# A fused convolution-attention and mixture-of-experts kernel: four taps a step, another plan for the last batch's expert tiles, and a combination that runs on into the tail

## The chip, the cores and the metric

The kernel runs on one core of a Trainium2 chip. Time is device time in microseconds of one execution; several executions are given by their median. The core has a matrix engine (TensorE; PE in the profile, its weight loads PEld), a vector engine (VectorE, DVE), an activation engine (ScalarE, ACT), GpSimd (POOL) and a queue processor (SyncE, SP) that issues most DMAs. Each engine works through its own instructions in the order in which the program lists them.

## The reference

The input x is 8 images of 256 channels, 32 x 32 pixels. Layer 0 is a deformable attention with a learned position bias; layer 1 is a token attention with sigmoid weights and a mixture of 8 experts, two per token:

```python
# layer 0, on the group-normalised image, residual added
q = gconv1x1(x, wq)
off = tanh(pointwise(gelu(depthwise_6x6_stride_4(q)))) * 4        # 36 taps
vgs = normalize(grid + off)                                       # 8 x 8 sample points
kv = grid_sample(x, vgs);  k, v = gconv1x1(kv, wk), gconv1x1(kv, wv)
pos = grid_q - vgs
bias = mlp3(sign(pos) * log1p(abs(pos)))                          # 2 -> 64 -> 64 -> 1, for 1024 x 64 pairs
out = softmax(q k / 8 + bias) v;  x = x + w_out out
# layer 1, on tokens (1024 a batch, 256 wide), each part on layer-normalised tokens
t = t + sigmoid(t Wq t^T) t
for the two best experts e of a token:  t = t + weight_e * (gelu(t w1[e]) w2[e])
```

## The kernel before

**The main loop.** The costliest part is the bias network: its second layer (`second_layer`, L486) and third layer (`third_layer`, L506) on TensorE, its first layer (`first_layer`, L468) on GpSimd and VectorE in turn, the rectifications on ScalarE and VectorE. The loop `for n in range(NB * TURNS)` (L1122) walks through it in 64 turns a batch, `b, i = divmod(n, TURNS)`, with two second layers a turn and a third layer every other turn. All other work is written as Python generators, and each turn takes a few steps from them. So the order of work on every engine is written out by hand, by these turns; `in_order` (L76) fixes it as the order in which each engine runs. Only the scatters of routed rows may change places, and only among themselves between two other instructions of their engine.

**What a turn steps, in this order.**
- `mix(b, i, 0)` (L1145): expert steps, ahead of the bias layers.
- The bias layers, and with them the preparation of the next block of bias inputs, eight turns a block (L1139 to L1161): `scale()` when `n % 8 == 3`, `second()` and `hold(0)` when it is 4, `hold(1)` when it is 6. `hold` copies half of the block into a PSUM tile (`held_nb`) that the first layer on VectorE reads; the tile `still` that holds it is also where the taps (`shared`) accumulate and where small statistics live.
- `side.step` (L1163): the softmax of this batch (`softmax`, L533) and the preparation of the next batch's image (`prep`, L241): group statistics, normalising, query projection, the 36 taps of the depthwise convolution as VectorE additions in PSUM (L286 to L295, three taps a step), GELU, offsets, the pair table `fd` sent to DRAM, sampling weights, transposes (L382), the sampling matmuls (L394), keys and values (L409 to L421).
- `advance(mains)` (L1171): one step of each running token attention. `attention(b, ...)` (L606) returns two generators. `upper` starts at turn 53 of its own batch, `rest` at turn 0 of the next batch. `rest` ends with routing (`route`, L812) and then 16 scatters (L793, indirect DMAs on GpSimd's queue) that put the rows into the slots of their experts; after the last it appends the batch's `experts` to the list `mixtures`.
- `mix(b, i, 1)` (L1172): expert steps, behind the others.
- `step(sums)` (L1173): one step of the oldest `combine` (L991).

**Experts and combination.** `experts(b, rt)` (L911) works in rounds of 256 slots: 12 rounds for batches 0 to 6 (two tiles of 128 slots each, possibly of two experts), 15 for batch 7 (tiles of 256). A round takes three steps: second layer of the round before last (L945), its bias (L950) and the DMA of the rows to `ys` (L951); then fetches of rows (`xl`, L925) and weights (L932) and the first layer of the round before (L966, L974); then the transposes of this round's rows (L985, L987). A batch of 12 rounds takes 41 steps; after the last, its `combine` is appended to `sums`. `combine` has 22 steps: steps 0 to 15 each gather the rows of one of two experts for 128 tokens (`gs`, L1019, an indirect DMA on GpSimd's queue, which needs all rows in `ys`), steps 3 to 18 add them with their weights on VectorE (L1011), and steps 8, 12, 16 and 20 transpose a quarter of the result on TensorE (L1002), copy it on ScalarE and send it out (L1005).

**When expert steps fall due** is in `mix` (L1095). In batches 2 to 6, the experts of the batch two before (b - 2) get a step at turn 26, two steps in each of the 13 odd turns of `ODD` (31 to 55) and one in the turn after each; the 41st comes at turn 9 of the batch after. In the last batch (b = 7) three steps (`whole()`, L1116) are taken at once after turn 9, in turns that are odd or divisible by three, until batch 5's experts are through; batch 6's start at turns 62 and 63.

**The tail** (L1176 to L1189) follows the last turn: a loop steps batch 7's `rest` until it has ended, and takes a `whole()` of batch 6's experts in odd iterations while no attention tiles run, and in each iteration from the second of the routing on. Then a loop over batch 7's experts takes `whole()` and one `step(sums)` an iteration, and a last loop takes what is left of `sums`.

Of the kernel before, what the change touches and what calls it, by code (L numbers as in the profile page):

```python
# [67 lines left out]
TURNS = STEPS // 2  # L68
# [35 lines left out]
def tile_conv_attn_hybrid(ctx: ExitStack, tc: tile.TileContext, x, par, qw, w1, w2_, cst, out):  # L104
    nc = tc.nc
    NB = x.shape[0]
# [16 lines left out]
    def big(name):  # L123
        return t8.tile([P, 2, N], F32, tag="t8", name=name)
# [21 lines left out]
    def xin(b):  # L146
        return x[b].rearrange("(k p) h w -> p k (h w)", p=P)
# [11 lines left out]
    def par_(name):  # L159
        return pr_[:, PAR[name]]  # L160
# [80 lines left out]
    def prep(b, xb, st):  # L241
# [44 lines left out]
        for t in range(KS * KS):  # L286
            ky, kx = divmod(t, KS)
            row = (26, 0, 9, 18, 27, 1)[ky]
            tap = qp[:, row : row + 8].rearrange("p r k x -> p (r k) x")[:, :, kx : kx + 29 : 4]
            if t == 0:  # L290
                nc.vector.tensor_scalar(oc, tap, dw[:, 0:1], par_("dwb"), ALU.mult, ALU.add)
            else:
                nc.vector.scalar_tensor_tensor(oc, tap, dw[:, t : t + 1], oc, ALU.mult, ALU.add)
            if t % 3 == 2:
                yield  # L295
        oa = one.tile([P, 2, 8, 8], F32, name="oa")
        nc.scalar.activation(oa.rearrange("p k y x -> p y k x"), oc.rearrange("p (y k) x -> p y k x", k=2), AF.Gelu)
# [134 lines left out]
    def terms(b, k, h, part):  # L432
        number = 4 * k + 2 * h + part
        fd = sts[b]["fd"].rearrange("k (s r) f -> k r s f", r=2)
        ta = abpool.tile([P, 16, 2, 32], F32, name="ta")
        nb = abpool.tile([P, 16, 2, 16], F32, name="nb")
        nc_ = abpool.tile([P, 2, 8, 16], F32, name="nc")
        taf = ta.rearrange("p s g x -> p s (g x)")
        nbf = nb.rearrange("p s g y -> p s (g y)")
        ss = slice(part * 16, (part + 1) * 16)  # L440
        for r in range(2):
            rs = slice(64 * r, 64 * r + 64)
            nc.sync.dma_start(out=taf[rs], in_=fd[k, r, ss, 0:64].partition_broadcast(64))
            nc.sync.dma_start(out=nbf[rs], in_=fd[k, r, ss, 64 + 32 * h : 96 + 32 * h].partition_broadcast(64))

        def scale():
            nc.scalar.activation(taf, taf, AF.Identity, bias=par_("cb1"), scale=par_("w1x"))
            nc.scalar.activation(nbf, nbf, AF.Identity, scale=nw1y)

        def second():  # L450
            cps = [psum("cp") for _ in range(2)]
            for r, g in ((0, 0), (1, 1), (0, 1), (1, 0)):
                rs, gs = slice(64 * r, 64 * r + 64), slice(64 * g, 64 * g + 64)
                nc.tensor.matmul(
                    cps[r][gs, 0:128], lhsT=par_("w2")[rs, gs], rhs=nb[rs, 1::2, g, :],
                    start=True, stop=True, tile_position=(64 * r, 64 * g),
                )
            for r in range(2):
                nc.scalar.activation(  # L459
                    nc_[:, r].rearrange("p s y -> p (s y)"), cps[r][:, 0:128], AF.Identity, bias=ncb2,  # L460
                )

        def hold(half):
            nc.scalar.copy(held_nb[:, 4 * half : 4 * half + 4], nb[:, 8 * half + 1 : 8 * half + 8 : 2])  # L464

        return (ta, nb, nc_, b, number), scale, second, hold

    def first_layer(terms_, n):  # L468
        ta, nb, nc_, of, number = terms_
        h1 = hpool.tile([P, 2, 16, W], F32, name="h1", bufs=6)  # L470
        a = ta[:, n].unsqueeze(2).to_broadcast([P, 2, 16, W])
        b = nb[:, n].unsqueeze(3).to_broadcast([P, 2, 16, W])
        if second_form(of, number, n):
            b = held_nb[:, n // 2].unsqueeze(3).to_broadcast([P, 2, 16, W])
            nc.vector.tensor_tensor(h1, a, b, ALU.max)  # L475
            return h1, nc_[:, :, n // 2]
        nc.gpsimd.tensor_tensor(h1, a, b, ALU.subtract)  # L477
        return h1, None

    def rectify(h1, nc_):  # L480
        if nc_ is None:
            nc.scalar.activation(h1, h1, AF.Relu)  # L482
# [542 lines left out]
    class Side:  # L1025
# [5 lines left out]
        def step(self, both=True):  # L1031
            busy = False
            if self.waiting and not (sorting and self.busy):
                busy = self.busy
                self.busy = next(self.waiting[0], None)
                if self.busy is None:
                    self.waiting.pop(0)
                    self.busy = True
            if self.left and both and not busy:
                self.left = next(self.prep, self) is not self  # L1040
# [21 lines left out]
    h2s, side = [], None  # L1062

    mains, mixtures, sums = [], [], []

    def place(t):
        b, s = divmod(t, STEPS)
        return b, s // 64, s // 32 % 2

    def logits(t):  # L1070
        b, k, h = place(t)
        ss = third_layer(sts[b], k, h, t // 4 % 8, h2s[:4])
        del h2s[:4]
        if ss is None:
            return None
        if (k, h) == (0, 0):
            os_[b] = big("o")
        if (k, h) == (1, 1):
            sts[b]["last"] = ss
        else:  # L1080
            return softmax(sts[b], k, h, ss, os_[b], psum)

    def residual(b):
        xres[b] = big("x")
        nc.sync.dma_start(out=xres[b], in_=xin(b))
# [8 lines left out]

    def mix(b, i, part):  # L1095
        of = mixtures[0][0] if mixtures else NB
        if b == NB - 1 and of >= b - 2:
            if part and (i >= TURNS - 2 if of == b - 1 else i > 9 and (i % 2 or i % 3 == 0)):
                whole()
        elif of == b - 2:  # L1100
            if not part:
                due = i in ODD
            else:
                due = i == 26 or i in ODD or i - 1 in ODD
            if due:
                step(mixtures)
        elif of == b - 3 and i == 9 and not part:
            step(mixtures)

    ODD = (31, 33, 35, 37, 39, 41, 43, 45, 47, 49, 51, 53, 55)  # L1110

    def step(what):
        if what and next(what[0][1], what) is what:
# [2 lines left out]
    def whole():  # L1116
        of = mixtures[0][0] if mixtures else NB
        for _ in range(3):
            if mixtures and mixtures[0][0] == of:
                step(mixtures)  # L1120

    for n in range(NB * TURNS):  # L1122
        b, i = divmod(n, TURNS)
        turn = i
        if i == 0:
            steps = iter(())
            if b + 1 < NB:
                xb = big("xb")
                nc.sync.dma_start(out=xb, in_=xin(b + 1))
                steps = prep(b + 1, xb, sts[b + 1])  # L1130
            side = Side(steps)
        if b == 0 and i in (8, 16):
            nc.sync.dma_start(
                out=xss[i // 8 - 1].rearrange("(t p) c -> p t c", p=P),
                in_=zero.unsqueeze(1).to_broadcast([P, ROWS // P, C]),
            )
        if i == 46:
            residual(b)
        coming_ = (n // 8 + 1) * 16  # L1139
        if coming_ < total and n % 8 == 0:  # L1140
            b_, k_, h_ = place(coming_)
            coming, scale, second, hold = terms(b_, k_, h_, coming_ // 16 % 2)
        if n % 8 == 6 and coming_ < total:
            table = coming
        mix(b, i, 0)  # L1145
        new = []
        if n + 2 < NB * TURNS:
            new = [first_layer(table, (2 * n + 4 + r) % 16) for r in range(2)]
        h1s += new
        h2s += [second_layer(*h1s.pop(0)) for _ in range(2)]  # L1150
        for h in new:
            rectify(*h)
        ready = n % 2 == 0 and n and logits(2 * n - 1)
        if coming_ < total:
            if n % 8 == 3:
                scale()
            elif n % 8 == 4:
                second()
                hold(0)
            elif n % 8 == 6:  # L1160
                hold(1)  # L1161
        if i > 4 and not (sorting and i % 2):
            side.step(i > (8 if b else 4))  # L1163
        if ready:
            side.waiting.append(ready)
        if i == 0 and b:
            mains.append((b, below))
        elif i == 53:
            above, below = attention(b, sts[b], os_.pop(b), {})
            mains.append((b, above))  # L1170
        advance(mains)  # L1171
        mix(b, i, 1)  # L1172
        step(sums)  # L1173
        if i == TURNS - 1:
            side.finish()
    logits(total - 1)  # L1176
    mains.append((b, below))
    n = sorted_ = 0
    while mains:
        advance(mains)  # L1180
        if sorted_ or not attending and n % 2:
            whole()
        sorted_ = sorted_ or sorting
        n += 1
    while mixtures:
        whole()
# [111 lines left out]
```

## Time and profile before

| what | us |
|---|---|
| median of 3 runs | 3100.75 |
| lowest, highest | 3093.69, 3102.71 |
| the profiled execution | 3095.55 |
| its span, first to last instruction | 3093.7 |
| TensorE busy in it | 2816.0 (91%) |
| VectorE, ScalarE | 1897.3, 1899.3 (61% each) |
| GpSimd | 1382.0 (45%) |
| mean granted TensorE clock | 0.979 of full |

A turn begins in the trace where TensorE begins a turn's 16 matmul records of line L490. By that, the batches begin at these times:

| batch | begins at, us | length, us |
|---|---|---|
| 0 | 72.8 | 256.4 |
| 1 | 329.2 | 323.6 |
| 2 | 652.8 | 358.3 |
| 3, 4, 5, 6 | 1011.1, 1370.6, 1730.2, 2089.8 | 359.6 each |
| 7 | 2449.3 | 372.7 |
| tail | 2822.0 | 271.7 |

How to read the profile: engines are busy or idle; idle time is put down to whatever ended it, written `<-engine tile line`. A waiting instruction holds up all later instructions of its engine. Idle time of an engine counts only where the work that ends last had to wait for it. The names in a row, `out<-in`, are those of the program's tiles.

### The profile page before, as it was taken

Reading aid. Unit: us, or ns where it says so; the run is one execution under the profiler, and the core shown is the slowest. Engines: PE = TensorE matmul, PEld = TensorE weight load, DVE = VectorE, ACT = ScalarE, POOL = GpSimd, SP = SyncE. Lnnn points to the kernel's source line nnn. Section 1 sums busy time; section 2 is a strip of 40 time slices with the busy share of each in tenths; the row PEclk is TensorE's granted clock in tenths of the full one; section 3 lists DMA queues with packets and bytes.
Section 4 is the critical chain, followed back from the end, with each engine's and each line's share of the span. In section 5 each row is a group of like instructions: output and inputs, shape, how many; then the busy total and the mean of one; then the engine's idle time right before and its main releaser. Section 6 shows DMA issues by size and latency. Waiting matters only on the chain. (4 is left out here: it accounts for less than half of the span.)

```text
span 3093.7 us, 51788 instructions
## 1 busy us (share of the span) xinstructions
PE 2816.0 (91%) x19592; PEld 1393.8 (45%) x19592; DVE 1897.3 (61%) x2968; ACT 1899.3 (61%) x2735; POOL 1382.0 (45%) x945
## 2 busy tenths in 40 slices
PE   3989998899999999999999999999999998989965
PEld 2223453334454454444445444554545455425754
DVE  4887667766765676656765567656775553593112
ACT  3776656666576656756576666766577665665322
POOL 2555434644344543545535464445435443472123
PEclk7999999999999999999999999999999999999988
DMA  3321111210373124712265124731256154433377
GB/s 102 89 46 35 21 28 28 60 38 15 103 209 100 42 65 133 208 47 57 81 175 155 48 57 111 215 91 44 64 142 201 32 147 141 129 93 96 120 232 225
DMA packets 428298, 311.23 MB, mean 101 GB/s; under 512 B 284432, under 2 KB 368656, under 8 KB 428048
## 3 DMA queue, kind: packets, MB, share of 16 engines
q1 hardware_dynamic: 415472, 273.14, 31.5%
q0 software_dynamic: 12288, 33.57, 3.4%
q8 instruction: 155, 2.54, 0.3%
q10 hardware_dynamic: 288, 1.20, 0.1%
q14 instruction: 95, 0.78, 0.1%
HBM read 239.93 MB, written 67.90 MB: 100 GB/s over the span
## 5 line engine op out<-in xcount | busy, mean ns | idle before, releaser
L477 POOL TENSOR_TENSOR h<-ta,nb 128x1024 f32<-128x1024 f32 x512 | 980.8, 1918 | 1123.3 <-PE h2p L490 1001.9
L490 PE MATMUL h2p<-h,pr__101 64*64 64x512 f32 x8192 | 1011.9, 605 | 82.0 <-DVE h L498 55.5
L496 ACT ACTIVATE h<-h2p,pr__101 128x1024 f32<-128x1024 f32 x512 | 570.9, 1115 | 485.8 <-PE h2p L490 485.4
L498 DVE TENSOR_TENSOR h<-h2p,nc 128x1024 f32<-128x1024 f32 x512 | 625.3, 1221 | 316.4 <-PE h2p L490 303.9
L475 DVE TENSOR_TENSOR h<-ta,still 128x1024 f32<-128x1024 f32 x512 | 620.1, 1211 | 46.8 <-ACT still L464 42.8
L482 ACT ACTIVATE h<-h 128x1024 f32<-128x1024 f32 x512 | 537.8, 1051 | 13.5 <-POOL h L477 13.2
L490 PEld LDWEIGHTS h2p<-h,pr__101 64*64 64x64 f32 x8192 | 254.4, 132 | 607.3 <-issue 284.1
L517 PE MATMUL sim<-h,pr__101 128*32 128x512 f32 x4096 | 496.6, 603 | 0.0
L950 DVE TENSOR_TENSOR yt<-yp,w 128x512 f32<-128x512 f32 x99 | 68.5, 692 | 379.6 <-PE yp L945 333.3
L517 PEld LDWEIGHTS sim<-h,pr__101 128*32 128x32 f32 x4096 | 107.5, 109 | 362.8 <-issue 362.7
L723 PE MATMUL ap<-qt,tn 128*128 128x256 f32 x1024 | 252.4, 390 | 4.1 <-ACT sg L741 2.6
L733 PE MATMUL vp<-tt,sg 128*128 128x256 f32 x1024 | 233.0, 381 | 3.6 <-ACT nc L459 3.3
L723 PEld LDWEIGHTS ap<-qt,tn 128*128 128x128 f32 x1024 | 185.7, 191 | 88.4 <-issue 40.4
L945 PE MATMUL yp<-w,ht 128*128 128x256 f32 x792 | 201.2, 398 | 25.5 <-ACT ht L974 7.0
L1019 POOL DMA_INDIRECT gs<-ys,slot x128 | 129.7, 1014 | 193.1 <-DVE xc L1011 51.5
L966 PE MATMUL hp<-xg,w 128*128 128x128 f32 (+1 forms) x1464 | 200.0, 289 | 12.1 <-ACT xg L987 4.4
L733 PEld LDWEIGHTS vp<-tt,sg 128*128 128x128 f32 x1024 | 193.5, 190 | 36.9 <-issue 5.7
L966 PEld LDWEIGHTS hp<-xg,w 128*128 128x128 f32 x1464 | 183.4, 193 | 45.7 <-issue 23.5
L745 DVE TENSOR_TENSOR x<-x,vp 128x512 f32<-128x512 f32 x64 | 44.0, 688 | 256.3 <-PE vp L733 256.3
L974 ACT ACTIVATE ht<-hp,w 128x128 f32<-128x128 f32 (+1 forms) x366 | 108.6, 377 | 146.7 <-PE hp L966 127.2
L945 PEld LDWEIGHTS yp<-w,ht 128*128 128x128 f32 x792 | 147.2, 196 | 61.4 <-ACT ht L974 13.9
L741 ACT ACTIVATE sg<-ap 128x512 f32<-128x512 f32 x128 | 76.5, 598 | 143.8 <-PE ap L723 131.9
(273 smaller groups left out, 2556.9 us busy)
## 6 DMA issues: line engine op xcount, KB each, us to landing
w<-in_w SPq DMA_DIRECT2D x183, 384.0 KB
w<-in_w SPq DMA_DIRECT2D x183, 257.0 KB
ta<-fd SPq DMA_DIRECT2D x128, 256.0 KB
xl<-xs SPq DMA_DIRECT2D x99, 256.0 KB
ys<-yt SPq DMA_DIRECT2D x99, 256.0 KB
nb<-fd SPq DMA_DIRECT2D x128, 128.0 KB
xb<-in_x SPq DMA_DIRECT2D x8, 1024.0 KB
x<-in_x SPq DMA_DIRECT2D x8, 1024.0 KB
```

What stands on the lines that cost most here:

```text
L475: nc.vector.tensor_tensor(h1, a, b, ALU.max)
L477: nc.gpsimd.tensor_tensor(h1, a, b, ALU.subtract)
L482: nc.scalar.activation(h1, h1, AF.Relu)
L490: nc.tensor.matmul(h2p[gs, r, :], lhsT=par_("w2")[rs, gs], rhs=h1[rs, g].rearrange("p y x -> p (y x)"), start=True, stop=True, tile_positi ...
L496: nc.scalar.activation(h2, h2p, AF.Relu, bias=par_("cb2"))
L498: nc.vector.tensor_tensor(h2.rearrange("p r (y x) -> p r y x", x=W), h2p.rearrange("p r (y x) -> p r y x", x=W), nc_.unsqueeze(3).to_broad ...
L517: nc.tensor.matmul(sim[32 * q : 32 * q + 32, :], lhsT=par_("z3")[:, 15 - m : 47 - m], rhs=h2s[2 * u + q // 2][:, q % 2, :], start=False, s ...
L723: nc.tensor.matmul(ap[:, u, :], lhsT=tn[:, k, m0 : m0 + P], rhs=qt[:, k, quarter(q)], start=(k == 0), stop=(k == 1),)
L733: nc.tensor.matmul(vp[:, i, :], lhsT=sgs[s][:, u, i * P : (i + 1) * P], rhs=tt[:, 2 * todo[n - 2 + s][1] + u, :], start=(s == u == i == 0) ...
L945: nc.tensor.matmul(yp[:, s, :], lhsT=ht[:, f, s * P : (s + 1) * P], rhs=f2[:, s * several // 2, f * C : (f + 1) * C], start=(f == 0), stop ...
L966: nc.tensor.matmul(hp[:, f, us], lhsT=f1[:, u, k * C + f * P : k * C + (f + 1) * P], rhs=xg[:, k, us], start=(k == 0), stop=(k == 1),)
L1019: nc.gpsimd.indirect_dma_start(out=got[m][:, c, :], out_offset=None, in_=yv[:, :], in_offset=bass.IndirectOffsetOnAxis(ap=slot[:, c, m : m ...
```

## The change

Four edits are made, and no instruction is added or taken away; only their order changes.

1. The taps of `prep` yield after every fourth tap, so that the 36 taps take 9 steps and no longer 12. `prep` gets no step in turns after 44 whose number is 3 or 4 modulo 8.
2. `hold(0)` is issued one turn later, in the turn with `n % 8 == 5`.
3. In the last batch `mix` follows the same pattern as in the others, with a list of its own, `LATE`: batch 4's last step comes at turn 1; batch 5's experts start with one step in turn 2, take steps at turns 3, 4, 7 and 8, and then the odd turns 35 to 55 and the ones after them, with the last step in turn 57. Batch 6's experts take no step in the main loop any more; they start in the tail.
4. The tail's first loop takes a `step(sums)` in each iteration. Batch 5's combination, which begins in turn 57, goes on there, and batch 6's begins there when its experts have ended.

```diff
@@ prep @@
-            if t % 3 == 2:
+            if t % 4 == 3:
                 yield
@@ mix @@
         of = mixtures[0][0] if mixtures else NB
-        if b == NB - 1 and of >= b - 2:
-            if part and (i >= TURNS - 2 if of == b - 1 else i > 9 and (i % 2 or i % 3 == 0)):
-                whole()
-        elif of == b - 2:
-            if not part:
-                due = i in ODD
-            else:
-                due = i == 26 or i in ODD or i - 1 in ODD
-            if due:
+        odd, first_, last = (LATE, 2, 1) if b == NB - 1 else (ODD, 26, 9)
+        if of == b - 2:
+            if i in odd or part and (i == first_ or i - 1 in odd) or b == NB - 1 and i == odd[-1] + 2 and not part:
                 step(mixtures)
-        elif of == b - 3 and i == 9 and not part:
+        elif of == b - 3 and i == last and not part:
             step(mixtures)
     ODD = (31, 33, 35, 37, 39, 41, 43, 45, 47, 49, 51, 53, 55)
+    LATE = (3, 7, 35, 37, 39, 41, 43, 45, 47, 49, 51, 53, 55)
@@ the main loop @@
             elif n % 8 == 4:
                 second()
+            elif n % 8 == 5:
                 hold(0)
             elif n % 8 == 6:
                 hold(1)
         if i > 4 and not (sorting and i % 2):
-            side.step(i > (8 if b else 4))
+            side.step(i > (8 if b else 4) and not (i > 44 and i % 8 in (3, 4)))
@@ the tail @@
         if sorted_ or not attending and n % 2:
             whole()
         sorted_ = sorted_ or sorting
+        step(sums)
         n += 1
```

## The prediction

> **What bounds the kernel now.** I read the page first, then the busy time by stage, then the engines' own timelines around the end. The page gives the share of each engine and its clock in 40 slices:
>
> ```profile
> PE   3989998899999999999999999999999998989965
> PEclk7999999999999999999999999999999999999988
> ```
>
> TensorE is at 9 tenths for nearly the whole span and at full clock, so in the eight batches time falls only where TensorE's idle time falls. The last two slices (6 and 5) lie outside that rule. I cut the trace into turns (a turn begins at every 16th second-layer matmul of L490 on TensorE) and asked for the busy time of five stretches, turns 0-8, 9-30, 31-34, 35-56 and 57-63. Columns: stretch, length, then busy us (and instructions) of PE, PEld, DVE, ACT, POOL, then clock, DMA share, GB/s. Batch 6, the pattern of batches 3 to 6:
>
> ```profile
> 2133.20:2258.90 125.70, 123.47 (x823) 60.45 (x822) 90.61 (x149) 77.78 (x104) 65.43 (x48) 1.00 0.25 65
> 2258.90:2283.60 24.70, 20.90 (x160) 9.62 (x156) 16.40 (x23) 16.66 (x25) 11.40 (x8) 1.00 0.60 164
> 2283.60:2414.40 130.80, 125.25 (x954) 68.47 (x953) 79.78 (x134) 91.34 (x150) 60.76 (x40) 1.00 0.60 175
> ```
>
> Batch 7, the same cuts from turn 9 on, then parts of the tail: up to the first scatter of routed rows, the scatters, the last experts, the last combination:
>
> ```profile
> 2492.70:2683.20 190.50, 173.50 (x1145) 106.85 (x1144) 82.26 (x117) 115.29 (x177) 66.02 (x49) 0.98 0.50 151
> 2683.20:2698.20 15.00, 14.62 (x115) 4.30 (x114) 13.30 (x17) 11.48 (x14) 12.44 (x9) 1.00 0.59 150
> 2698.20:2793.10 94.90, 79.33 (x620) 23.95 (x616) 82.85 (x120) 60.17 (x75) 67.20 (x48) 0.98 0.29 81
> ...
> 2959.60:2986.60 27.00, 8.95 (x42) 6.43 (x41) 2.15 (x5) 3.35 (x10) 17.57 (x18) 0.67 0.65 213
> 2986.60:3061.10 74.50, 66.08 (x307) 54.30 (x308) 14.41 (x27) 20.54 (x46) 13.37 (x14) 0.96 0.85 267
> 3061.10:3093.70 32.60, 6.58 (x24) 3.29 (x21) 9.87 (x21) 3.52 (x6) 15.89 (x16) 0.55 0.51 154
> ```
>
> Two things are to be seen. Batch 7 squeezes the experts of batch 5 between the attention tiles of turns 11-30 and leaves TensorE idle 17.0 us there, and then idles 15.6 us of the 94.9 us of turns 35-56, where nothing but the bias layers is left. And in the tail there are 27 us in which GpSimd alone works: it issues 16 scatters, and batch 7's experts can't start before the last.
>
> **Part A, the last batch's experts (gain).** Counting the steps of the generators by hand: batch 5's rounds now start at turns 2-8 (first fetch, one hidden layer, two transposes), rest, and take the odd turns 35-55 with the even ones after, ending in turn 57. Each stretch, built from batch 6's where the same work stands:
> - Turns 0-8: 43.4 now, plus transposes 2 x 0.60 and one first layer 1.95 = 46.6.
> - Turns 9-30: batch 6's 125.7, less its preparation of a next image, which batch 7 lacks (four L277 matmuls at 0.65 and two small ones, about 3.0) = 122.7.
> - Turns 31-34: batch 7's own 15.0.
> - Turns 35-56: batch 6's 130.8, less preparation (sampling matmuls 3.84, transposes 4 x 0.60, keys and values about 1.5, and a 1.6 wait that they cause), plus the last second layer 1.99 = 123.5.
> - Turns 57-63: 28.9, plus 1.0 because GpSimd's first gather of batch 5 now waits there for the last expert rows = 29.9.
>
> Sum 337.7 against 372.7; I take **-34**. The bound on the small side: if none of the 15.6 us idle were filled, turns 35-56 would cost 94.9 plus 11 rounds of 1.99 + 1.95 + 0.60, plus 1.99 = 146.8, and the gain is -12. The other bound is -38 (batch 7 has 22 table loads of ScalarE against batch 6's 13, 1.28 us each; fewer switches may fill more).
>
> **Part B, preparation in batches 0 to 6 (small gain).** Four taps a step shorten the 36 taps from 12 steps to 9; everything behind moves three steps earlier (GELU from turn 32 to 29, sampling transposes from turns 47-53 to 42-48, the sampling matmuls from turn 54 to 50), and from turn 45 on no step falls on turns 51, 52, 59, 60, where ScalarE also scales the terms. It adds and removes no instruction. TensorE's waits in batch 6:
>
> ```profile
> PE h2p L490 <- DVE h L498: 2.9, 2, 1.8
> PE tp L985 <- ACT nc L459: 2.0, 2, 1.5
> PE at__21334 L558 <- ACT nc L459: 1.6, 1, 1.6
> ```
>
> The 2.9 are turns 31-32, behind the last taps and GELU; the 1.6 is turn 52, behind transposes' copies; 0.7 more waits for a sampling copy (xt). That is 7.2 us with the 2.0. Against it: a fourth tap (0.454 us) on turns where VectorE is full (5.4 us of turn 24's 5.7), GELU's own wait (16.2 us in 8, 2 us each) moved to turn 29, and 2.1 us more ScalarE in turn 44 (5.5 of 7.0 busy). I take -1.5 a batch, **-10** for seven, bounds -25 (half of the 7.2 gone each time) and +8 (nothing gained, 1.1 lost each). Moving hold(0) one turn later costs nothing by itself: a 0.28 us copy in a turn with less ScalarE work; VectorE's 42.8 us of waits for that line lie in the same bounds.
>
> **Part C, the tail up to the attention tiles (small gain).** Batch 6's experts started at turns 62-63 and stood at round 5 when the tiles begin (2879.0); now two rounds fewer (2 x 4.5 = 9.1) stand there, and three output transposes of batch 5's combination come in (3 x 0.65). -7 if TensorE sets this stretch, 0 if the last softmax does; I take **-4**, bounds -7 to +3 (nine gathers of 1.27 us ahead of one `pow` on GpSimd's queue).
>
> **Part D, the scatters (loss).** The added step(sums) in the tail's loop puts batch 6's gathers between batch 7's scatters: counted by hand, scatters 1-3, gather 1, scatter 4, gather 2, and so on to scatter 16. GpSimd takes them in order. In batch 7's turn 9 the trace shows what the first gather of a batch waits for (its row issue on the DMA queue, then GpSimd):
>
> ```profile
> 2493.60 0.38 SPq L951 DMA_DIRECT2D ys<-yt  x1
> ```
> ```profile
> 2496.53 1.04 POOL L1019 DMA_INDIRECT gs<-ys,slot  x1 [4.06 <-PE h2p L490]
> 2497.60 1.93 POOL L477 TENSOR_TENSOR h<-ta,nb 128x1024 f32<-128x1024 f32 x1
> ```
>
> It starts 2.93 us after the last expert rows are sent, and the GpSimd work behind it stands still. In the tail of before, the fourth and the last scatter were free of that:
>
> ```profile
> 2963.52 0.97 POOL L793 DMA_INDIRECT xs<-ut,slot  x1 [0.31 <-issue]
> ...
> 2978.84 0.97 POOL L793 DMA_INDIRECT xs<-ut,slot  x1 [0.31 <-issue]
> ```
>
> Batch 6's last rows left at 2971.4, when it mattered to no one. With two rounds more to go (issues at 2948.6, 2954.9, 2960.3: 5.8 us a round) they leave at 2983.1, so the first gather starts at 2986.0 and the fourth scatter at 2987.3 instead of 2963.5: +23.8. Then 12 more gathers at 1.27 us lie between the rest: +15.2. Behind the waiting gather: 13 scatters, and behind the last one the fetch, the experts and the whole end. TensorE has nothing to hide it. Sum **+39**. Bounds: +16.5 (no wait, 13 x 1.27) and +46 (rounds of 7.6 us, as from 2963.1 to 2970.7, and gathers of 1.5).
>
> [...] Here a gather beside VectorE's additions took 1.18 us (at 3071.24) against 0.95 alone. [...]
>
> **Part E, the end (small gain).** Batch 7's 15 rounds come every 4.8 us, with batch 6's combination between them, and every 4.4 where it is missing least (3056.7 to 3061.1); eight rounds are now free of it: -2.4. At the very end, the first addition waited until 3069.6 for a load queued behind two output writes of batch 6, now gone: -1. **-3.4**, bounds -6 and 0.
>
> **Sum.** -34 - 10 - 4 + 39 - 3.4 = -12.4. On the profiled execution (3095.55, span 3093.7 and 1.9 around it) that is 3083.2; on the median of the runs, 5.2 higher, 3088.4. I say **3086**.
>
> **Rivals.**
> - **The scatters are not held** (gathers find the rows landed, only their 16.5 us remain): -12.4 - 22.5 = -35, about 3063 (midway between the two bases, as for all that follow). For it: the change gives the gathers 27 us in which little else runs. Against it: the order of the steps and the wait above.
> - **The second half doesn't absorb the rounds**: half of the way to Part A's bound, -25, and Part B -5: -25 - 5 - 4 + 39 - 3.4 = +2, about 3100; with A at -12 it is +15, 3113. For it: ScalarE waits (`nc`) in turns 44-52. Against it: batch 6 does the same with preparation on top, at 5.6 us idle.
> - **Slower: the hole in the tail is longer than forecast.** Place: between scatters 3 and 16. In turns 44-47 of batch 7, where both kinds already alternate, a scatter follows the scatter before it after 4.4 us (there a bias layer lies between); with that spacing 13 pairs cost 3.1 more than 1.28 each, +40 in place of +15.2, sum +13, 3111. It decides from +61 for Part D.
> - **The change does no more than shift** (all parts near nothing): within 0.3%, in the second rival's share.
>
> **Chances.** Forecast 0.50 (3077 to 3097), not held 0.12, not absorbed 0.25, longer hole 0.13. About 0.3% (9.3 us) is what a measurement of this kernel can tell from no change. The forecast lies mostly below 3091.4 (0.40 of its 0.50), the first rival wholly, 0.02 of the second: faster 0.54. Same: 0.10 of the forecast and 0.18 of the second: 0.28. Slower: 0.05 of the second and the third: 0.18. Range 3062 to 3110: from the first rival to just short of the third.
>
> **What would show it.** Right: the main loop ends some 44 us earlier; in the tail one gather with a long idle time before it after the third scatter, then strict alternation, and an idle stretch of TensorE of more than 40 us. Part A is wrong if turns 35-56 of batch 7 take over 130 us; Part B if batches 2 to 6 don't get shorter than 358; Part D if the first scatter and the last lie less than 35 us apart. The forecast fails most easily where A and D, both large, don't cancel as worked out.

## The result, and the profile after

The change makes no measurable difference: 3099.13 us (median of 12 runs, 3090.63 to 3103.45) against 3097.22 for the kernel before (12 runs, 3088.94 to 3102.71), ratio 1.0008 with a 95% interval of 0.9999 to 1.0017. The forecast said 3086, 0.4% faster; the time lies inside its range (3062 to 3110, wide enough for faster, same and slower), but the sign of the likeliest case didn't come: "faster" had 0.54 of the chances, "same" 0.28. The profiled execution of after has a span of 3095.5 us, 1.8 longer than before. Almost nothing moved in the sum, and almost everything moved inside it:

| stretch | before, us | after, us | difference | forecast |
|---|---|---|---|---|
| batches 0 to 6 (Part B) | 2376.5 | 2380.0 | +3.5 | -10 |
| batch 7 (Part A) | 372.7 | 338.9 | -33.8 | -34 |
| end of main loop to first scatter (Part C) | 137.6 | 130.8 | -6.8 | -4 |
| first to last scatter (Part D) | 19.2 | 56.8 | +37.6 | +39 |
| last scatter to the end (Part E) | 114.9 | 116.5 | +1.6 | -3.4 |

The sum is +2.1; the main loop begins 0.3 earlier, which makes the +1.8 of the spans.

The page's slices show the exchange at once: the two 8s that batch 7 had (slices 34 and 36) are 9s now, and the last four slices fall from 9, 9, 6, 5 to 8, 8, 4, 5.

```profile
PE   3889998899999999999999999999999999998845
PEclk7999999999999999999999999999999999999968
```

The busy time by stretch of batch 7 (turns 9-30, 31-34, 35-56), then first scatter to batch 7's first hidden layer, the last experts, the last combination (columns as in the prediction: length, then busy us and instructions of PE, PEld, DVE, ACT, POOL, then clock, DMA share, GB/s):

```profile
2498.70:2620.70 122.00, 119.49 (x809) 58.67 (x808) 72.32 (x101) 76.20 (x102) 57.79 (x42) 1.00 0.23 55
2620.70:2637.70 17.00, 16.65 (x130) 5.68 (x126) 12.51 (x16) 12.02 (x15) 10.27 (x6) 1.00 0.17 41
2637.70:2761.80 124.10, 119.70 (x905) 63.50 (x904) 77.19 (x121) 78.55 (x127) 57.01 (x37) 1.00 0.61 179
2922.20:2988.00 65.80, 19.35 (x101) 14.32 (x101) 9.89 (x20) 7.23 (x21) 31.28 (x32) 0.68 0.61 198
2988.00:3063.20 75.20, 65.75 (x304) 53.97 (x304) 11.51 (x18) 20.50 (x46) 0.00 (x0) 0.96 0.73 223
3063.20:3095.50 32.30, 5.42 (x16) 2.74 (x16) 7.53 (x17) 2.34 (x4) 15.34 (x16) 0.53 0.45 139
```

TensorE's idle time in turns 9 to 56 of batch 7 fell from 32.9 us to 7.3. What was gained there is given back in the fourth row: 65.8 us in which TensorE works 19.35. GpSimd's timeline of after in that hole shows why (start, length, engine, line, operation, tiles, and in brackets the idle time before it and what ended it):

```profile
2924.85 0.96 POOL L793 DMA_INDIRECT xs<-ut,slot  x1 [0.30 <-issue]
2946.97 0.98 POOL L1019 DMA_INDIRECT gs<-ys,slot  x1 [21.16 <-DMA xc<-xu]
2948.26 0.99 POOL L793 DMA_INDIRECT xs<-ut,slot  x1 [0.31 <-issue]
2949.55 0.98 POOL L1019 DMA_INDIRECT gs<-ys,slot  x1 [0.30 <-issue]
2950.83 0.98 POOL L793 DMA_INDIRECT xs<-ut,slot  x1 [0.31 <-issue]
...
2979.05 0.97 POOL L793 DMA_INDIRECT xs<-ut,slot  x1 [0.30 <-issue]
```

After the third scatter the queue stands for 21.16 us in front of batch 6's first gather; then gathers and scatters alternate every 1.28 us. The row names `xc` as the releaser, but the DMA queue of SyncE tells which event mattered: the issue of the last expert rows ends at 2944.2, and the gather follows 2.75 us after that; in the prediction's rows of turn 9 it was 2.55.

```profile
2938.63 5.59 SPq L951 DMA_DIRECT2D ys<-yt  x2
2944.40 0.90 SPq L1016 DMA_DIRECT2D xc<-xu  x2
```

### The profile page after: what moved, and what is told of

It reads as the page before. It is cut to its first block, busy times and chain, and to the rows that moved or that the text cites. A ratio compares the mean times of both kernels' runs of the same rounds, so it can differ in the third digit from the quotient of the medians.

```text
span 3095.5 us, 51726 instructions
## 1 busy us (share of the span) xinstructions
PE 2814.5 (91%) x19592; PEld 1391.9 (45%) x19592; DVE 1932.1 (62%) x2968; ACT 1872.0 (60%) x2715; POOL 1381.3 (45%) x945
## 5 line engine op out<-in xcount | busy, mean ns | idle before, releaser
L966 PE MATMUL hp<-xg,w 128*128 128x128 f32 (+1 forms) x1464 | 202.0, 291 | 12.5 <-ACT xg L987 3.5
L974 ACT ACTIVATE ht<-hp,w 128x128 f32<-128x128 f32 (+1 forms) x366 | 108.2, 376 | 133.3 <-PE hp L966 126.3
```

The lines of the kernel that those rows point to most:

```text
L966: nc.tensor.matmul(hp[:, f, us], lhsT=f1[:, u, k * C + f * P : k * C + (f + 1) * P], rhs=xg[:, k, us], start=(k == 0), stop=(k == 1),)
```

## The experiments

All experiments start from the kernel after or the one before, as their diffs say. Single runs scatter by several us, so where a run has no interval, its profile's stretches are read instead. The theory to begin with: the gain of the last batch is real, and the hole between the scatters eats it. The rivals: the hole's time is lost anyway, because the experts of batch 6 or the loads need it; and the small gain that is missing comes from edits 1 and 2.

### 1. Batch 5's combination in the tail's loop, batch 6's not

```diff
-        step(sums)
+        if sums and sums[0][0] == NB - 3:
+            step(sums)
```

> The change as it is, but the tail's first loop steps the combination of batch 5 alone; batch 6's starts with batch 7's experts, as before the change. My theory (the last batch gained 34 us, and the gathers between the scatters took 37.6 of it back): the scatters come 1.28 us apart again, 19 us from first to last in place of 56.8, the end after them keeps its 115-117 us, and the time falls by 37 to 38 us to a span of about 3058 (ratio to the kernel before 0.988). Rival 1 (the tail's experts of batch 6, two rounds later, set the end, and not the gathers): the span from the last scatter to the end grows by the 12 us or more of these rounds, and the time falls by less than 25 us. Rival 2 (the combination must be done somewhere and costs the same where it goes): no change of time.

Measured: 3076.74 us against 3094.24, ratio 0.9935 (0.9922 to 0.9947); span 3075.8. The first and the last scatter lie 19.1 apart, as expected. But against after the end comes only 19.7 us earlier, where the hole was worth 37.6; the main loop of this execution is 6.3 longer than after's, which makes it 26.0. From the last scatter to the end it takes 126.7 us, 10.2 more than in after. So the gathers between the scatters did cost what the change gained, but a part of the hole is lost to something else. SyncE's and VectorE's timelines of this run show it (scatters from 2930.0 to 2949.1):

```profile
2928.41 2.65 SPq L932 DMA_DIRECT2D w<-in_w  x3
2934.20 7.18 SPq L932 DMA_DIRECT2D w<-in_w  x4
2947.76 7.13 SPq L932 DMA_DIRECT2D w<-in_w  x4
...
2964.42 0.90 SPq L925 DMA_DIRECT2D xl<-xs  x2
```
```profile
2933.66 0.69 DVE L950 TENSOR_TENSOR yt<-yp,w 128x512 f32<-128x512 f32 x1 [3.90 <-issue]
2952.75 0.69 DVE L950 TENSOR_TENSOR yt<-yp,w 128x512 f32<-128x512 f32 x1 [18.40 <-remote]
2958.02 0.69 DVE L950 TENSOR_TENSOR yt<-yp,w 128x512 f32<-128x512 f32 x1 [3.74 <-PE yp L945]
```

Batch 6's last rounds now run beside the 16 scatters. SyncE takes 7.2 us to issue four weight loads there, and one round's addition comes 19.1 us after that of the round before, where the next comes after 5.3. The fetch of batch 7's rows (`xl`) is queued behind batch 6's last rows, and so comes at 2964.4, 15 us after the last scatter; in before it stood right behind it. The first rival has a part of the truth.

### 2. One gather alone between the scatters

```diff
-        step(sums)
+        if sums and (sums[0][0] == NB - 3 or first_one):
+            first_one = sums[0][0] == NB - 3
+            step(sums)
```

> As the first kernel, but the first step of batch 6's combination, with one gather and one load, stays behind the third scatter. It tells the wait from the alternation. My theory puts 21.2 us on the wait of that one gather for the last expert rows and 12.8 x 1.28 = 16.4 us on the others: from the first scatter to the last 19.2 + 22.4 = about 41.5 us, span about 3080. Rival (the alternation itself slows GpSimd, the wait is hidden by something else): under 25 us from first to last scatter.

Measured: 3086.29 us (one run; before on the same chip 3094.24), 41.4 us from the first scatter to the last, the forecast to a tenth. GpSimd's timeline of this run:

```profile
2932.27 0.96 POOL L793 DMA_INDIRECT xs<-ut,slot  x1 [0.30 <-issue]
2954.54 0.99 POOL L1019 DMA_INDIRECT gs<-ys,slot  x1 [21.31 <-DMA xc<-xu]
2955.83 0.98 POOL L793 DMA_INDIRECT xs<-ut,slot  x1 [0.30 <-issue]
2957.12 0.96 POOL L793 DMA_INDIRECT xs<-ut,slot  x1 [0.30 <-issue]
```

So Part D splits as the prediction had it: 22.3 for the wait and its one gather, and the other 15.4 (56.8 - 41.4) for 12 gathers of 1.28.

### 3. Gathers whose rows have long landed, between the scatters

Batch 5's combination is held until the scatters start, batch 6's stays behind them; the routing tiles get a third buffer, since batch 5's slots now live longer.

```diff
+            return small.tile(list(shape), dtype, name=name, bufs=2 if name == "expert" else 3)
...
-        step(sums)
+        if sums and sums[0][0] == NB - 3 and sorted_ and not sorting:
+            step(sums)
```

> As the first kernel, but batch 5's combination is held from the last turn on until the scatters begin, so that its remaining gathers (9 of 16, whose rows have long landed) lie between the scatters; the slots and weights of the routing have three buffers in place of two, so that this can be. It prices a gather without a wait: my theory says 9 x 1.28 = 11.5 us more from first to last scatter than 19.2, about 31, and a span of some 3069; rival (any gather between two scatters makes the next wait for its transfer, some 2 us): 40 us or more.

Measured: 3079.98 us (one run), 39.4 from the first scatter to the last, 8.4 more than expected. GpSimd's timeline names the difference:

```profile
2921.45 1.00 POOL L793 DMA_INDIRECT xs<-ut,slot  x1 [0.30 <-issue]
2931.37 0.96 POOL L1019 DMA_INDIRECT gs<-ys,slot  x1 [8.93 <-PE tp L985]
2932.64 0.99 POOL L793 DMA_INDIRECT xs<-ut,slot  x1 [0.30 <-issue]
2933.93 0.97 POOL L1019 DMA_INDIRECT gs<-ys,slot  x1 [0.30 <-issue]
```

The nine gathers cost 9 x 1.28 = 11.5 again, but one of them waited 8.93 us for something else than its rows (the row names a transpose of TensorE; I read it as a buffer of the combination, which isn't shown by more than this row). Even with its rows long landed, a gather in the scatters' queue brings its own issue, and in this one run one of the nine also brought a wait.

### 4. No combination in the tail's loop at all

```diff
+            return small.tile(list(shape), dtype, name=name, bufs=2 if name == "expert" else 3)
...
-        step(sums)
```

> The change without the added step of the combinations in the tail's first loop (with three buffers for slots and weights). Batch 5's remaining 15 steps then stand beside batch 7's experts, and nearly all of batch 6's 22 behind them. My theory: scatters 19 us from first to last, but 15 more gathers of 1.26 us at the end, +19 to +22 us there: span about 3077 to 3081. Rival 2 of the first kernel (the combination costs the same anywhere): 3095.

Measured: 3083.7 us (one run, span 3081.9 where 3077 to 3081 were expected), worse than the first experiment. The scatters start 10.0 us earlier than in the first experiment (4.8 of it the main loop of that execution) and take 19.1. But batch 6's last rows come 35.3 us after the first scatter (33.7 in the first experiment), and what was left out of the tail's loop stands at the end: from the last expert rows to the end it takes 40.1 us with 20 gathers, not before's 31.9 with 16. SyncE's timeline has the slow loads beside the scatters (2920.0 to 2939.1) again:

```profile
2919.98 1.57 SPq L932 DMA_DIRECT2D w<-in_w  x2
...
2924.21 7.16 SPq L932 DMA_DIRECT2D w<-in_w  x4
```

By these stretches batch 5's combination belongs into the tail's loop, and batch 6's doesn't.

### 5 to 8. Edits 1 and 2, together and taken apart

Each starts from the kernel before. 5 has both edits; 6 has the four taps alone, 7 the taps and the pause of the preparation, 8 the later `hold(0)` alone:

```diff
-            if t % 3 == 2:
+            if t % 4 == 3:
...
+            elif n % 8 == 5:
                 hold(0)
...
-            side.step(i > (8 if b else 4))
+            side.step(i > (8 if b else 4) and not (i > 44 and i % 8 in (3, 4)))
```

> The kernel before with edits 1 and 2 alone (four taps a step, no preparation in turns 3 and 4 of a block after turn 44, first hold a turn later); the last batch and the tail as before. Theory 'Part B is those two edits': the batches without a clock window have the lengths of after, 361.2 for batches 3 to 6, 357 to 358 for batch 2, 316 for batch 1, 259 for batch 0; batches 0 to 6 together 3.5 us longer than before (a 3.4 us half-clock window adds 1.7 wherever one falls). Batch 7 as before (372.7), first to last scatter 19.2. Rival 'the other plan of the last batch and the tail lengthens the batches before it, through code or memory that the program lays out otherwise': batches 3 to 6 stay at 359.6.

> The kernel before with four taps a step alone; preparation goes on in all turns, the first hold stays where it was. Theory 'the taps' shift makes the new waits' (GELU to turn 29, sampling to turns 42 to 50): batches 3 to 6 at 360.5 to 361.5 where no clock window falls, batch 1 about 6 us shorter than before (nothing but preparation bounds it). Rival 'the taps gain what I forecast (1.5 a batch), and the pause or the hold loses it': batches 3 to 6 at 358.

> The kernel before with the whole of edit 1 (four taps a step, and no preparation in turns 3 and 4 of a block after turn 44), the first hold where it was. By the theory that the taps make the new waits: within 0.5 of the taps alone, since the pause takes ScalarE work off two turns of a block and puts it on others. Rival 'the pause is what pays': 1 us a batch shorter than the taps alone.

> The kernel before with edit 2 alone (the first half of the next block held one turn later). Forecast in the record: costs nothing by itself. Theory as forecast: batches 3 to 6 at 359.6 within 0.3, the others as before. Rival 'the hold, now next to the other one and later, makes VectorE's first layer and so TensorE wait': batches 3 to 6 1 us or more longer, and the wait of TensorE for ScalarE or VectorE at the turns of a block's end grows.

Measured, lengths of batches in us, with the number of 3.4 us stretches at half clock (see the last part) in brackets where there are any:

| kernel | batch 0 | batch 1 | batch 2 | 3 to 6, the clean ones |
|---|---|---|---|---|
| before | 256.4 (1) | 323.6 (2) | 358.3 (1) | 359.6 |
| after | 258.9 (2) | 315.8 (1) | 357.8 | 361.1 to 361.2 |
| 5: both edits | 258.9 (2) | 315.7 (1) | 357.9 | 361.0 to 361.2 |
| 6: taps alone | 257.5 (1) | 317.0 (1) | 357.7 | 361.0 to 361.1 |
| 7: taps, pause | 257.5 (1) | 315.8 (1) | 357.8 | 361.1 |
| 8: hold alone | 256.7 (1) | 322.6 (2) | 357.1 | 359.9 to 360.1 |

With both edits alone the clean batches are those of after, to 0.2 us, so Part B is theirs and the last batch's plan has nothing to do with it; batch 7 (371.2, two half-clock stretches; before 372.7, three) and the scatters (19.2) are as in before. The taps alone lengthen each of the batches 3 to 6 by 1.45 us and shorten batch 1, which has no experts to fill its turns, by 6.6 (one half-clock stretch fewer is in that). The pause changes nothing there (0.1). The hold costs 0.3 to 0.5 by itself, a little more than the nothing that was forecast; on top of the taps and the pause it adds nothing (5 against 7). The single runs (3094.62, 3092.27, 3095.62, 3097.02, before 3096.37) can't tell these apart.

TensorE's waits in batch 3 of the taps alone (us in total, times, longest) stand against the list of before in the prediction, and VectorE and TensorE in turn 33 show one of them being made:

```profile
PE h2p L490 <- DVE h L498: 1.9, 2, 1.7
PE tp L985 <- ACT at L571: 1.8, 1, 1.8
PE at__11110 L558 <- ACT nc L459: 1.7, 1, 1.7
PE fp L339 <- ACT nc L459: 1.5, 1, 1.5
```
```profile
1179.08 0.75 DVE L320 SCALAR_TENSOR_TENSOR gk<-gk,cs 128x256 f32<-128x256 f32 x2
1179.75 2.00 DVE L323 SCALAR_TENSOR_TENSOR gk<-gk,cs 128x128 f32<-128x128 f32 x1
1181.79 1.45 DVE L324 TENSOR_SCALAR gk<-gk 128x640 f32<-128x640 f32 x1
...
1184.60 1.22 DVE L498 TENSOR_TENSOR h<-h2p,nc 128x1024 f32<-128x1024 f32 x1
...
1185.88 1.09 PE L490 MATMUL h2p<-h,pr__101 64*64 64x512 f32 x8 [1.67 <-DVE h L498]
```

Turns 31 and 32 lost their waits behind the taps, as forecast, 2.5 us of TensorE's idle time. But the offset arithmetic, 4.2 us of VectorE in turn 32, came forward with everything else; VectorE works without a gap from 1179.1 on, and its rectification in turn 33 is late by TensorE's 1.67. The 1.5 in front of a transpose of the experts (turn 36) is still there, in front of `fp` now; the 1.6 of turn 52 stayed, although the transposes that I had blamed for it left; and turn 46 has a new 1.8. TensorE's idle time in batch 3 went from 14.7 to 15.7 us, and its busy time from 344.9 to 345.3; turns 33 and 46 added 1.7 and 1.5 us of idle time.

The new waits have something in common: VectorE instructions that take longer in their new turns. In before the offset arithmetic takes 1.6 us and stands in turn 36, where GpSimd has just finished; with the taps alone it starts while GpSimd is at work. In turn 46 it is an instruction of the routing (L898), and behind it the first layer, the second hold's copy and the `at` copy that TensorE waits for. Before, then the taps alone:

```profile
1212.76 0.28 DVE L323 SCALAR_TENSOR_TENSOR gk<-gk,cs 128x128 f32<-128x128 f32 x1
1263.50 0.33 DVE L898 TENSOR_TENSOR still<-ends,cs 128x168 f32<-128x168 f32 x1
```
```profile
1179.52 2.09 POOL L477 TENSOR_TENSOR h<-ta,nb 128x1024 f32<-128x1024 f32 x1 [0.41 <-PE h2p L490]
1181.56 1.32 POOL L691 TENSOR_TENSOR x<-x,ut 128x512 f32<-128x512 f32 x1
1258.52 2.72 DVE L898 TENSOR_TENSOR still<-ends,cs 128x168 f32<-128x168 f32 x1
1259.10 1.92 POOL L477 TENSOR_TENSOR h<-ta,nb 128x1024 f32<-128x1024 f32 x1
```

L323 ends 0.15 us after the GpSimd instruction beside it, L324 0.35 and L898 0.22. In batches 2 to 6 of the three kernels with three taps a step (before, 8 and 10) L323, L324 and L898 take 0.28, 0.49 and 0.33 us; in all nine kernels with four taps 2.00, 1.45 and 2.5 to 2.7. That their length makes the two waits is read from the rows; no run moved these instructions alone.

### 9. Batch 6's experts at turns 62 and 63 again

The first experiment, with the old start of batch 6's experts put back into `mix`:

```diff
         elif of == b - 3 and i == last and not part:
             step(mixtures)
+        elif b == NB - 1 and of == b - 1 and part and i >= TURNS - 2:
+            whole()
```

> The kernel after with batch 6's combination taken out of the tail's loop, as in the first experiment, and batch 6's experts starting at turns 62 and 63 again, as before the change. Theory 'what the first experiment lost beside the scatters were the two rounds by which batch 6's experts start later': the last rows of batch 6 leave within 25 us of the first scatter, batch 7's first hidden layer comes 164 to 166 us after the end of the main loop (171.9 in the first experiment), the end 5 to 7 us earlier than there: ratio to before 0.991 to 0.993, span near 3070. Rival 'the rounds beside the scatters are slow whatever their number' (a round takes 10 to 12 us there): batch 7's experts start as in the first experiment, 171 to 172 after the main loop, ratio 0.9935 as there or a little more, since turns 62 and 63 get longer.

Measured: 3070.01 us against 3096.93, ratio 0.9906 (0.9891 to 0.9922); span 3070.1, the number expected. Batch 6's last rows are added up 9.4 us after the first scatter (2946.2 and 2936.8), so the fetch of batch 7's rows is waiting when the last scatter comes; batch 7's first hidden layer stands 167.2 us after the main loop, 1 to 3 us later than forecast and 4.7 earlier than in the first experiment. SyncE's timeline (scatters from 2936.8 to 2955.9):

```profile
2932.86 3.92 SPq L932 DMA_DIRECT2D w<-in_w  x4
2936.89 0.50 SPq L951 DMA_DIRECT2D ys<-yt  x1
2938.22 1.70 SPq L932 DMA_DIRECT2D w<-in_w  x2
...
2958.44 0.87 SPq L925 DMA_DIRECT2D xl<-xs  x2
```

The rival's number (171 to 172) falls: with nearly all loads issued ahead of the scatters, no round takes 10 us. Whether a round with all its loads beside the scatters would still be slow, this run doesn't test. The early start has a price ahead of the scatters, where the two rounds now stand: 139.6 us from the main loop to the first scatter, 7.3 more than in the first experiment; from there to the end it takes 133.3, 12.5 less. Batch 7 has the same length with the early start as without (340.6 in both, one half-clock stretch in each).

### 10. The same, with edits 1 and 2 undone

```diff
-            if t % 4 == 3:
+            if t % 3 == 2:
...
-            elif n % 8 == 5:
                 hold(0)
...
-            side.step(i > (8 if b else 4) and not (i > 44 and i % 8 in (3, 4)))
+            side.step(i > (8 if b else 4))
```

> As the kernel with the early start, and with edits 1 and 2 undone (three taps a step, no pause, first hold where it was). By the theory that edits 1 and 2 cost 3.5 us in batches 0 to 6 and nothing behind them: 3.5 us less than the early start alone, a ratio 0.0011 lower, and batches 3 to 6 back at 359.6. Rival 'the new plan of batch 7 needs the pause and the earlier sampling': batch 7 itself isn't touched by the taps (it prepares no image), so only the hold can speak there; then batch 7 gets 1 us or more longer than 339.

Measured: 3064.75 us against 3096.93, ratio 0.9899 (0.9885 to 0.9914). The difference to the run before it, 0.0007, is smaller than either interval, so the times alone don't show it. The batches do: 3, 4 and 6 are back at 359.6, and batches 0 to 6 without their half-clock stretches (1.7 us each, an estimate: half of 3.4) sum to 2368.5 against 2372.3, 3.8 less where 3.5 were expected. (The 3.5 holds one such stretch more in after than in before; without them before and after lie 1.8 apart, so the two pairs of profiles put edits 1 and 2 at 2 to 4 us.) Batch 7 is as long with the old hold as with the new one (338.9 each without such stretches), so the rival falls. This has the lowest median of all versions, 1% below the kernel before, with an interval that leaves no doubt of the sign.

## Why the prediction came out as it did

- **Part A was right, by its stretches too.** 46.2, 122.0, 17.0, 124.1, 29.6 us against the 46.6, 122.7, 15.0, 123.5, 29.9 of the working. The stretches of batch 6 with the same work were the right ruler, and ScalarE's table loads (1.28 us each) did not get in the way: they fell from 22 to 10. The stretches of the working sum to -35.0, of which the forecast took -34. Of the 33.8, 25.6 are idle time of TensorE.
- **Part B is the step that failed**: "I take -1.5 a batch", -10. Experiments 5 to 8 put +1.45 a batch on the four taps. The waits behind the taps went, as forecast. But the working put a change in the length of the moved instructions at nothing, without asking what they would stand beside: VectorE's L323, L324 and L898, 1.1 us together, take 6.2 where they now fall beside GpSimd's instructions, and TensorE waits in turns 33 and 46, which the working had not looked at. The bounds (-25 to +8) held the +3.5, of which 1.7, by the same estimate, is one more half-clock stretch. What the working left out on the other side is batch 1, about 5 to 6 us shorter, where preparation alone sets the length.
- **Part C**: -6.8, near its lower bound of -7: TensorE sets that stretch, not the softmax. It is the time of two rounds that stand elsewhere now, and no gain by itself: in experiment 9, with the rounds back, the stretch takes 139.6 (before 137.6).
- **Part D was right, in size and in its two terms.** The fourth scatter came 22.1 us late (forecast 23.8), the other 12 gathers cost 15.5 (forecast 15.2). The rows that were expected at 5.8 us a round came a little sooner. The 13 gathers took 0.97 to 0.99 us each; the 1.18 us of before's gather at 3071.24, beside VectorE's additions, isn't seen in these rows. VectorE is busy in only a sixth of this hole (9.9 of 65.8), and beside the gathers it runs nothing but the combination's additions, so what other VectorE work would do to a gather was not shown.
- **Part E is the second step that failed**: "eight rounds are now free of it: -2.4". From the first hidden layer to the last rows it took 75.2 us before, with the combination beside, and 75.3 after, with none in the second half. A round comes every 4.8 us on average in both: two times 1.9 us of matmuls, 0.6 of transposes, up to 0.6 of waiting for ScalarE's `ht`, and now and then a wait for weights (4.4 us in all after, 2.8 before). The combination lies beside that chain, not on it: in the other runs, with 15 or 16 gathers between the last scatter and the last rows, the stretch takes 74.1 to 74.9 us (80.4 in experiment 4, whose first rounds are slow themselves). The term was also mis-sized by its own figures: 4.8 less 4.4 us in eight rounds is 3.2, not 2.4. The 1 us at the very end didn't come either: the end's long wait is for another load of `xc`, 4.94 us at 3088.46 after and 4.29 before.

So the sum missed by 14.2 us (-12.4 forecast, +1.8 measured), 13.5 of it in Part B and 5.0 in Part E against it, and 4.2 the other way in C and D. By the signs that the prediction set itself, the one gather with its long wait and the strict alternation came as described, but the main loop ended 30.6 us earlier and not some 44, and batches 3 to 6 didn't get shorter than 358. "GpSimd alone works" in the 27 us of before's tail was a misreading of its own row, in which TensorE is busy for 8.95 us: these were mostly batch 6's last rounds, which experiment 1 brought to light. Of the rivals, "the second half doesn't absorb the rounds" gave the best number, 3100, by luck and for a wrong reason: the second half absorbed them all. (Its -25 isn't half of the way from -34 to -12 either; that would be -23, and 3102.) "Not held", 3063, didn't happen, and closing the hole altogether isn't worth its length either: 3099.1 - 37.6 would be 3061.5, and experiment 1 came to 3076.7, since batch 6's late rounds were hidden in the hole and came to light when it closed; with their early start back the time was 3070.0, and without edits 1 and 2 also 3064.8. "A longer hole" fell: 1.28 us an instruction, not 2.2.

**What is left open.** What makes the waits of turns 33 and 46, and why those of turns 52 and 36 stayed, was read from rows, and not tried by moving single steps. The 0.4 us by which TensorE's busy time in batch 3 grew was not followed. What slows SyncE beside a run of scatters (last part) wasn't taken apart. And in experiment 3 the 8.93 us wait has only the one row that names it.

## What to carry to other kernels

An instruction that waits in an in-order queue is priced by what stands behind it: here 21 us of wait and 13 issues of 1.28 us stood in front of the scatters that start the end, and ate a gain of 34. Before filling such a hole from the other side, ask what lies hidden in it: the late rounds cost nothing as long as the hole was there, and some 6 us in all without it. And when a chain is moved to an earlier turn to remove a wait, add up the engines in the turns in which it lands, and see what will run beside it: a wait that goes is a gain only if the next in line isn't as late, and an instruction need not keep its length (here 0.28 us became 2.00).

## What the runs showed of the hardware

**TensorE's granted clock halved behind stretches with short waits.** In the traces it falls to a half (0.50 to 0.53 in the rows below) for 3.4 us or a multiple of that (6.8 us from 528 us on in before), so the main loops are read here in stretches of 3.4 us. In the twelve profiles' main loops (after 330 us) there are 60 stretches (or pairs of them) at half clock, and each follows a stretch in which TensorE was busy for 57% or less. Of the stretches with at most 45%, 34 of 36 were followed by one; of some 200 between 45% and 57%, 26; above 57%, none. Two pairs in before's batch 7, and one in after's batch 6 whose first stretch holds the 1.46 us wait for `fp` in turn 36:

```profile
2572.70:2576.10 3.40, 1.19 (x6) 0.90 (x7) 1.94 (x10) 3.26 (x5) 0.00 (x0) 0.99 0.65 209
2576.10:2579.50 3.40, 3.40 (x11) 2.81 (x10) 0.49 (x1) 0.00 (x0) 0.00 (x0) 0.51 0.00 0
2610.20:2613.60 3.40, 0.77 (x9) 0.19 (x5) 1.01 (x1) 2.00 (x3) 0.00 (x0) 1.00 0.45 156
2613.60:2617.00 3.40, 3.40 (x8) 2.74 (x9) 0.00 (x0) 2.08 (x3) 0.00 (x0) 0.50 0.00 0
```
```profile
2290.40:2293.80 3.40, 1.94 (x19) 1.16 (x16) 0.36 (x2) 2.65 (x5) 0.00 (x0) 1.00 0.53 151
2293.80:2297.20 3.40, 3.40 (x12) 2.04 (x14) 0.48 (x1) 0.33 (x1) 0.00 (x0) 0.53 0.10 25
```

After's batches 4 and 6, with one such stretch each, take 362.7 us, batches 3 and 5, with none, 361.1 to 361.2: 1.5 to 1.6 each. Where they fall differs from profile to profile (the table of experiments 5 to 8 counts them), and the clock goes with the scatter of the times: of the 12 runs of after, the fastest (3090.63 us) has a mean granted clock of 0.979, the slowest (3103.45) one of 0.975. They are also a part of Part A: in the five profiles with the old plan of the last batch, batch 7 holds 2 or 3 of them (before 3, some 5 us by the estimate of 1.7 each), in the seven with the new plan 0 or 1; TensorE idles 25.6 us less in after's batch 7 than in before's. In after's batch 6, 1.46 us of idle time inside one stretch stood ahead of one of them; by these rows a wait of that size can have a second price of some 1.6 us.

**Loads issued beside a run of scatters were slow on the issuing side.** Four weight loads took SyncE 7.1 to 7.2 us to issue in experiments 1 and 4, while 16 scatters ran, and 3.8 to 4.1 ahead of them or at their start: 3.79, 3.78 and 4.09 in before (at 2944.71, 2951.00 and 2956.10), 3.92 in experiment 9. Four in before took 6.11 with no scatter beside them (at 2930.53), 2.35 of it one gap ahead of the third load. In the trace of experiment 1, single steps of SyncE that take 0.02 to 0.4 us elsewhere take 0.7 beside the scatters; in before, three steps of 0.02 to 0.04 us elsewhere took 0.70 each from 2982.93 on, 3 us behind the last scatter. In after, only three scatters stood beside the loads (four in 4.01 us at 2925.62), and loads within the first 3 us of a run of scatters kept their pace (experiment 9: two in 1.70 us).

**Two VectorE instructions took longer when a GpSimd instruction was under way.** The instruction of L323 stands 96 times in the twelve traces. In 40 of them no GpSimd instruction that started ahead of it was still running, and it took 0.28 to 0.29 us; in the other 56 it took 1.36 to 2.00 us and ended 0.15 us after the GpSimd instruction. For L324 it is 48 times at most 0.50 us, and 48 times 1.44 us or more, ending 0.35 us after. Not every instruction does so: L898 in before, at 1263.50, began 0.01 us after a GpSimd addition of 2.10 us and took 0.33.
